# Layer 1's inverse square roots as powers on GpSimd, and a new order of the kernel's end (a two-layer graph network on one core)

## The chip, the core and the metric

The kernel runs on one core of a Trainium2 chip. The metric is the time of one execution on the device, in microseconds, and the figure given for a kernel is the median of its runs. A core has TensorE (PE, matrix products), VectorE (DVE), ScalarE (ACT), GpSimd (POOL) and SyncE (SP). Each works through its own queue of instructions in order, and an instruction that waits holds up all that stand behind it in that queue.

## What is computed

There are 4096 nodes with 64 features, an adjacency matrix of 4096 x 4096 zeros and ones, and two layers. Cut to what matters:

```python
def layer0(x):                      # a weighted sum of the neighbours
    rank = cumsum(mask, axis=1);  deg = rank[:, -1:];  k = minimum(deg, 100)
    pos = rank - (deg - k)
    w = mask * where(pos > 0, 0.5 ** (k - pos), 0.0)
    return w @ (x @ weight) + bias

def layer1(x):
    h = (adj @ x + x) / (sum(adj, axis=1) + 1)
    out = relu(concat([x, h], axis=1) @ W + b)
    return out / maximum(norm(out, axis=1), 1e-12)

x = layernorm(x + layer0(x))        # layernorm: (y - mean) / sqrt(var + 1e-5)
x = layernorm(x + layer1(x))
```

Layer 1 needs two inverse square roots for each node: one of the sum of squares of its `out` (the norm), and one of the variance of its row (the layernorm).

## The kernel before

**Tiles and stages.** The nodes are cut into eight slabs of 512 rows (four blocks of 128). The first 220 us or so are a pipeline over all (slab, k) pairs: it loads the adjacency in pieces of 128 x 4 x 512, counts neighbours, makes the weights of layer 0 and gathers; in between it finishes layer 0 for the slab before, and takes the parts of layer 1's sums whose rows are ready. The order within it is written out with hooks. The end, everything from `gather(*held)` (line 666) on, is written out by hand as a list of calls; a call puts its instructions into the queues of its engines, in the order of the list.

**The end.** Layer 1 is finished by units: slabs 5 and 2 (called 5_2), then 0 and 1 (0_1), 4 and 3 (4_3), slab 6, and slab 7 in two halves, 7a and 7b. For a slab, `own` (line 548) or `own_half` (553) runs TensorE over the remaining blocks of its sum, one matrix product for each. Then, for a unit:

- `last_hT` (563), for slab 7 `half_hT` (570): the sum is taken out of PSUM to hT, on VectorE where a stored part has to be added (L566), otherwise on ScalarE (L573).
- `last_pz` (588): TensorE multiplies hT by the weights (L594).
- `last_z` (596): VectorE adds the part of layer 1 that was computed before, c1 (L601).
- `last_sq` (603): the squares of relu(z), on ScalarE in two steps (L608, L609) or on VectorE in one (L611).
- `last_ss` (613): VectorE sums them (L616) and takes the larger of that and a floor (L618); ScalarE takes the square root (`root_a`, L364).
- `last_rn` (621): VectorE refines the root and inverts it (`root_b`): four small instructions, L370, L371, L373, L374.
- `last_y` (625): y = relu(z) times the inverse norm on VectorE (L630), plus x1 on GpSimd or VectorE (L633).
- `last_mv` (635): the mean and variance of y on VectorE (L382, L384); ScalarE takes the square root (L364).
- `last_r` (640): `root_b` again; with ScalarE next, VectorE also forms the offset, minus mean times inverse root (L646).
- `last_o` (648): the normalised rows, on ScalarE (L655, one instruction for each block of 128 rows) or VectorE (L659), and the store by SP (L664).

The two halves of an inverse root, as they stand before:

```python
s = sqrt(v + eps)                       # root_a, ScalarE
q = 1 / (s * s + eps + v)               # root_b, VectorE, three instructions
r = (s * 2.0) * q                       # root_b, VectorE, the fourth
```

**What ties the units together.** Most tiles of the end (hT, z, sq, y, and the small ones) have two buffers that units take in turn, so the third unit waits until the first has been read for the last time: y of 7a takes over the buffer of y of 4_3. GpSimd has no work in the end but its additions of x1. Its queue holds the loads of the adjacency before that.

Of the kernel before, what the change touches and what calls it, by code (L numbers as in the profile page):

```python
# [9 lines left out]
F32 = mybir.dt.float32  # L10
# [6 lines left out]
ALU = mybir.AluOpType  # L17
# [7 lines left out]
P = 128  # L25
R = 512
TB = R // P
# [6 lines left out]
LN_EPS = 1e-5  # L34
# [6 lines left out]
def adj_resnorm_kernel(  # L41
# [26 lines left out]
    nc = tc.nc  # L68
    D = w0.shape[0]
    NG, NK = adjT.shape[0], adjT.shape[1]  # L70
    NB = NK * KB
# [4 lines left out]
    const = ctx.enter_context(tc.tile_pool(name="const", bufs=1))  # L76
# [5 lines left out]
    small = ctx.enter_context(tc.tile_pool(name="small", bufs=2))  # L82
# [8 lines left out]
    for g in range(NG):  # L91
        n = 1 if g == 0 else 2 if g < 4 else 4
# [56 lines left out]
    zero = const.tile([P, 1], F32, name="zero")  # L149
    nc.vector.memset(zero, 0.0)  # L150
    eps_ln = const.tile([P, 1], F32, name="eps_ln")
# [36 lines left out]
    part = {}  # L188
    deg = const.tile([P, NB], F32, name="deg")
    least = const.tile([P, NB], F32, name="least")  # L190
    x1T = const.tile([D + 1, R], F32, name="x1T")
    nc.vector.memset(x1T[D : D + 1, :], 1.0)

# [112 lines left out]
    def second(acc, g, b, first, last):  # L306
        nc.tensor.matmul(acc, lhsT=x1hl[:, b, :], rhs=A[g][b // KB][:, b % KB, :], start=first, stop=last)  # L307
# [51 lines left out]
    ep = {}  # L359

    def root_a(v, eps, name):

        s = small.tile([P, v.shape[1]], F32, tag="s", name=f"s_{name}")
        nc.scalar.activation(s, v, AF.Sqrt, bias=eps)  # L364
        return s

    def root_b(s, v, eps, name):

        q = small.tile([P, v.shape[1]], F32, tag="q", name=f"q_{name}")
        nc.vector.tensor_tensor(q, s, s, ALU.mult)  # L370
        nc.vector.scalar_tensor_tensor(q, q, eps, v, ALU.add, ALU.add)  # L371
        r = small.tile([P, v.shape[1]], F32, tag="r", name=f"r_{name}")
        nc.vector.reciprocal(q, q)  # L373
        nc.vector.scalar_tensor_tensor(r, s, 2.0, q, ALU.mult, ALU.mult)  # L374
        return r

    def moments(y, name):
        n = y.shape[1]
        st = small.tile([P, n, 6], F32, tag="st", name=f"st_{name}")
        mv = small.tile([P, n, 2], F32, tag="mv", name=f"mv_{name}")  # L380
        for t in range(n):
            nc.vector.bn_stats(st[:, t, :], y[:, t, :])  # L382
        for t in range(n):
            nc.vector.bn_aggr(mv[:, t, :], st[:, t, :])  # L384
        return mv
# [122 lines left out]
    for c, chunk in enumerate(chunks):  # L508
        ahead = chunks[c + 1] if c + 1 < len(chunks) else []
        n, m = len(chunk), len(ahead)  # L510
# [5 lines left out]
        for (g, k), share in zip(chunk, shares):  # L516
# [7 lines left out]
            w = weigh(g, k, nr) if i == 0 else None  # L524
            for s in share:
                count(*s, s == ahead[0], s == ahead[-1])
            w = w or weigh(g, k, nr)
# [18 lines left out]
    a_half, b_half = slice(0, R // 2), slice(R // 2, R)  # L546

    def own(g, b0, b1):

        for b in range(b0, b1):  # L550
            second(acc[g], g, b, b == have[g] * KB, b == NB - 1)

    def own_half(rows, b0, b1):
        for b in range(b0, b1):
            nc.tensor.matmul(
                acc[L, rows.start],
                lhsT=x1hl[:, b, :],
                rhs=A[L][b // KB][:, b % KB, rows],
                start=b == 0,
                stop=b == NB - 1,  # L560
            )

    def last_hT(g):
        ep["hT", g] = epi.tile([P, R], F32, tag="hT", name=f"hT1_{g}")
        if g in part:
            nc.vector.tensor_tensor(ep["hT", g], acc[g], part[g], ALU.add)  # L566
        else:
            nc.scalar.copy(ep["hT", g], acc[g])

    def half_hT(rows):  # L570
        if rows.start == 0:
            ep["hT", L] = epi.tile([P, R], F32, tag="hT", name=f"hT1_{L}")
        nc.scalar.copy(ep["hT", L][:, rows], acc[L, rows.start])  # L573
# [22 lines left out]
    def last_z(u):  # L596

        name, bs = u
        z = ep["z", name] = epi.tile([P, len(bs), D], F32, tag="z", name=f"z_{name}")
        for t, c in spans(bs):  # L600
            nc.vector.tensor_tensor(z[:, t, :], ep["pz1", name][:, t, :], c1[:, c, :], ALU.add)  # L601

    def last_sq(u, on_act):
        name, bs = u
        z = ep["z", name]
        sq = ep["sq", name] = epi.tile([P, len(bs), D], F32, tag="sq", name=f"sq_{name}")
        if on_act:
            nc.scalar.activation(sq, z, AF.Relu)  # L608
            nc.scalar.activation(sq, sq, AF.Square)  # L609
        else:  # L610
            nc.vector.scalar_tensor_tensor(sq, z, 0.0, z, ALU.max, ALU.mult)  # L611

    def last_ss(u):
        name, bs = u
        ss = ep["ss", name] = small.tile([P, len(bs)], F32, tag="ss", name=f"ss_{name}")
        nc.vector.tensor_reduce(ss, ep["sq", name], AX.X, ALU.add)  # L616
        for t, c in spans(bs):
            nc.vector.tensor_tensor(ss[:, t], ss[:, t], least[:, c], ALU.max)  # L618
        ep["sn", name] = root_a(ss, zero, f"n_{name}")

    def last_rn(u):
        name, bs = u
        ep["rn", name] = root_b(ep["sn", name], ep["ss", name], zero, f"n_{name}")

    def last_y(u, on_pool):
        name, bs = u
        n = len(bs)
        y = ep["y1", name] = epi.tile([P, n, D], F32, tag="y", name=f"y1_{name}")
        rn = ep["rn", name].unsqueeze(2).to_broadcast([P, n, D])
        nc.vector.scalar_tensor_tensor(y, ep["z", name], 0.0, rn, ALU.max, ALU.mult)  # L630
        engine = nc.gpsimd if on_pool else nc.vector
        for t, c in spans(bs):
            engine.tensor_tensor(y[:, t, :], y[:, t, :], x1[:, c, :], ALU.add)  # L633

    def last_mv(u):
        name, bs = u
        mv = ep["mv1", name] = moments(ep["y1", name], f"l1_{name}")
        ep["s1", name] = root_a(mv[:, :, 1], eps_ln, f"l1_{name}")

    def last_r(u, on_act):  # L640
        name, bs = u
        mv = ep["mv1", name]
        r = ep["r1", name] = root_b(ep["s1", name], mv[:, :, 1], eps_ln, f"l1_{name}")
        if on_act:
            off = ep["off", name] = small.tile([P, len(bs)], F32, tag="off", name=f"off_{name}")
            nc.vector.scalar_tensor_tensor(off, mv[:, :, 0], -1.0, r, ALU.mult, ALU.mult)  # L646

    def last_o(u, on_act):
        name, bs = u
        y, mv, r = ep["y1", name], ep["mv1", name], ep["r1", name]  # L650
        o = wp.tile([P, len(bs), D], F32, tag="w", name=f"o_{name}")
        for t in range(len(bs)):
            if on_act:
                off = ep["off", name]
                nc.scalar.activation(  # L655
                    o[:, t, :], y[:, t, :], AF.Identity, bias=off[:, t : t + 1], scale=r[:, t : t + 1]
                )
            else:
                nc.vector.tensor_scalar(  # L659
                    o[:, t, :], y[:, t, :], mv[:, t, 0:1], r[:, t : t + 1], ALU.subtract, ALU.mult  # L660
                )
        for t, c in spans(bs):
            g, c0 = divmod(c.start, TB)
            nc.sync.dma_start(out=out[g][:, c0 : c0 + c.stop - c.start, :], in_=o[:, t, :])  # L664
# [36 lines left out]
    u = unit(5, 2)  # L701
# [3 lines left out]
    last_sq(u, True)  # L705
    last_hT(0)
    last_ss(u)
    own(1, 16, NB)
    last_rn(u)
    last_hT(1)  # L710
    last_y(u, True)
    own(4, 16, 24)

    v = unit(0, 1)
    last_pz(v)
    own(4, 24, NB)
    last_z(v)
    last_sq(v, True)
    last_mv(u)
    last_ss(v)  # L720
    last_hT(4)
    last_r(u, True)
    last_o(u, True)
    acc[3] = acc_of(3, "acc0")
    own(3, 12, NB)
    last_rn(v)
    last_y(v, True)
    last_hT(3)
    acc[6] = acc_of(6, "acc1")
# [2 lines left out]
    u = unit(4, 3)  # L732
    last_pz(u)
    last_mv(v)
    last_z(u)
    last_sq(u, True)
    last_r(v, True)
    last_ss(u)
    last_o(v, True)
    own(6, 20, NB)  # L740
    last_rn(u)
    last_y(u, True)
    last_hT(6)
    acc[L, 0] = acc_of(L, "acc0", R // 2, "7a")
    own_half(a_half, 0, NB // 2)
    last_mv(u)

    v = unit(6)
    last_pz(v)
    own_half(a_half, NB // 2, NB)  # L750
    last_r(u, True)
    last_z(v)
    last_sq(v, False)
    last_ss(v)
    half_hT(a_half)
    last_o(u, True)
    last_rn(v)
    last_y(v, True)
    acc[L, R // 2] = acc_of(L, "acc1", R // 2, "7b")
    own_half(b_half, 0, NB // 2)  # L760

    u, w = half_unit(0), half_unit(1)
    last_pz(u)
    own_half(b_half, NB // 2, NB)
    last_z(u)
    last_sq(u, False)
    last_ss(u)
    last_mv(v)
    last_rn(u)
    last_y(u, False)  # L770
    half_hT(b_half)
    last_pz(w)
    last_r(v, True)
    last_o(v, True)
    last_z(w)
    last_sq(w, False)
    last_ss(w)
    last_mv(u)
    last_rn(w)
    last_y(w, False)  # L780
    last_r(u, True)
    last_o(u, True)
    last_mv(w)
    last_r(w, False)
# [34 lines left out]
```

## Time and profile before

| what | us |
|---|---|
| median of 3 runs | 272.93 (272.83 to 273.19) |
| the profiled execution, whole | 273.33 |
| its span, first to last instruction | 271.5 |
| TensorE busy | 237.3 (87% of the span) |
| VectorE busy | 176.3 (65%) |
| ScalarE busy | 157.9 (58%) |
| GpSimd busy | 61.9 (23%) |

The profile is that of one execution. Busy time is a sum over the whole span; a line of the slices gives the busy share of an engine in each fortieth of the span, in tenths. A line of the timeline gives the start in us, the busy time in us, the engine, the line of the kernel, the operation, what it writes and what it reads, shapes, and how many instructions are merged; in brackets stands how long the engine had been idle before, and what released it. Names lose their slab numbers where the profile cuts them, so that "y" or "z" can be any unit; 7a and 7b keep theirs. The chain of work that ended last is followed back from the last instruction to what released each step; "issue" in it is time in which an engine waited for nothing that the profile shows.

### The profile page before, as it was taken

What the parts mean: (1) busy time and instruction counts of PE and PEld (TensorE: products, weight loads), DVE (VectorE), ACT (ScalarE), POOL (GpSimd) and SP (SyncE); (2) the same over time, 40 slices, a digit from 0 to 9 for tenths busy, and PEclk for the clock granted to TensorE, in tenths of its full rate; (3) what the DMA queues carried; (4) which work ended last, traced back from release to release, by engine and by line L of the source; (5) the groups of instructions that cost most, each with busy time, mean ns of one, the idle gap of its engine ahead of it and who ended that gap; (6) DMA issues with size and microseconds to landing.
All of it is one profiled execution on the core that took longest, in us unless ns stands there. A gap on an engine that the chain in (4) does not pass through costs nothing.

```text
span 271.5 us, 4838 instructions
## 1 busy us (share of the span) xinstructions
PE 237.3 (87%) x1865; PEld 105.0 (39%) x1865; DVE 176.3 (65%) x480; ACT 157.9 (58%) x226; POOL 61.9 (23%) x111
## 2 busy tenths in 40 slices
PE   8397688979899999999899999999998999997820
PEld 2122124334434343443344344434343546555710
DVE  5566634875596778367846684576577456597884
ACT  4456627897798869768854463436545322146351
POOL 8565551231101320322122121210200000221100
PEclk9979959999999999999999999999999999999985
DMA  6999999999997999799999999990500000010010
GB/s 97 195 230 234 241 212 214 222 214 214 223 214 141 165 211 214 124 171 214 182 179 205 203 162 180 168 168 12 98 2 0 0 2 0 0 42 20 19 58 21
DMA packets 12072, 37.13 MB, mean 137 GB/s; under 512 B 2066, under 2 KB 3218, under 8 KB 12050
## 3 DMA queue, kind: packets, MB, share of 16 engines
q0 software_dynamic: 10128, 35.66, 68.1%
q1 hardware_dynamic: 1922, 1.18, 1.5%
q8 instruction: 14, 0.23, 0.3%
q14 instruction: 8, 0.07, 0.1%
HBM read 69.34 MB, written 1.05 MB: 259 GB/s over the span
## 4 chain that ended last, share of the span: by engine, by line
PE 51%; DVE 11%; ACT 8%; issue 3%; POOL 1%; DVEq 0%; POOLq 0%; ACTq 0%
PE acc L298 10%; PE acc_part L307 9%; PE v L270 8%; PE v L280 5%; ACT w L287 4%; PE acc_right L307 3%; DVE w L288 3%; PE cnt L237 3%; PE vb L307 3%; PE pu L447 2%; PE va L307 2%; PE pz L594 2%; PE pz L395 2%; DVE x L422 1%; ACT a L320 1%
## 5 line engine op out<-in xcount | busy, mean ns | idle before, releaser
L288 DVE TENSOR_SCALAR w<-v 128x1024 int16<-128x1024 f32 x64 | 78.2, 1222 | 45.3 <-PE v L280 45.2
L287 ACT ACTIVATE w<-v,less 128x1024 int16<-128x1024 f32 x64 | 71.3, 1114 | 56.9 <-PE v L280 39.9
L298 PE MATMUL acc<-w,xhl 128*128 128x512 bf16 x256 | 67.2, 385 | 2.4 <-ACT hT L389 2.1
L109 POOL DMA_DIRECT2D a<-in_adjT_dram x65 | 35.5, 548 | 122.1 <-PE acc_part L307 49.9
L270 PE MATMUL v<-a,tri 64*64 64x512 bf16 x512 | 42.0, 397 | 4.3 <-ACT w L287 2.6
L298 PEld LDWEIGHTS <-xhl 128*128 128x128 f16 x256 | 23.9, 99 | 32.5 <-issue 9.5
L320 ACT CAST a<-a 128x1024 fp8e4<-128x1024 bf16 x32 | 33.3, 1039 | 0.0
L307 PEld LDWEIGHTS <-x1hl 128*128 128x128 f16 x224 | 19.8, 98 | 27.0 <-issue 5.7
L307 PE MATMUL acc_part<-a,x1hl 128*128 128x512 bf16 x108 | 28.0, 381 | 1.8 <-ACT x1hl L434 1.3
L247 DVE TENSOR_TENSOR cs<-cnt,cs 128x512 bf16<-128x512 f32 x20 | 13.8, 691 | 20.5 <-PE cnt L237 20.4
L237 PE MATMUL cnt<-a,pick 128*32 128x512 bf16 x256 | 21.9, 399 | 6.0 <-DMA a<-in_adjT_dram 6.0
L280 PE MATMUL v<-near,mine 32*128 32x512 bf16 x256 | 25.7, 391 | 0.2 <-ACT near L257 0.2
L270 PEld LDWEIGHTS <-tri 64*64 64x64 bf16 x512 | 12.6, 106 | 30.2 <-issue 28.0
L257 ACT ACTIVATE near<-rep,most 128x512 bf16<-128x512 f32 x28 | 19.1, 682 | 3.8 <-PE rep L255 3.7
L633 POOL TENSOR_TENSOR y<-y,x 128x256 f32<-128x256 f32 x7 | 5.0, 726 | 56.1 <-DVE y L630 56.1
L280 PEld LDWEIGHTS <-mine 32*128 32x128 bf16 x256 | 6.5, 91 | 24.9 <-issue 24.9
L255 PE MATMUL rep<-cs,further 128*128 128x512 bf16 x28 | 11.2, 400 | 3.7 <-DVE cs L247 1.7
L307 PE MATMUL acc_right<-a,x1hl 128*128 128x512 fp8e4 (+1 forms) x56 | 12.7, 379 | 0.0
L237 PEld LDWEIGHTS <-pick 128*32 128x32 bf16 x256 | 4.6, 94 | 19.8 <-issue 11.5
L655 ACT ACTIVATE o<-y,off,r_l 128x64 f32<-128x64 f32 x28 | 9.7, 428 | 3.1 <-issue 1.7
L382 DVE BATCH_NORM_STATS2 st_l<-y 128x6 f32<-128x64 f32 x60 | 9.0, 214 | 0.7 <-POOL y L633 0.6
L427 ACT CAST x1hl<-x 128x256 f16<-128x256 f32 x8 | 3.2, 406 | 10.1 <-DVE x L422 10.1
(139 smaller groups left out, 238.6 us busy)
## 6 DMA issues: line engine op xcount, KB each, us to landing
a<-in_adjT_dram POOLq DMA_DIRECT2D x63, 512.0 KB, 9.7
c<-in_x_pairs_dram POOLq DMA_DIRECT2D x8, 128.0 KB, 11.6
x<-in_x_dram POOLq DMA_DIRECT2D x8, 128.0 KB, 7.9
out_dram<-o SPq DMA_DIRECT2D x7, 128.0 KB, 1.7
a<-in_adjT_dram POOLq DMA_DIRECT2D x2, 256.0 KB, 4.7
out_dram<-o_7a SPq DMA_DIRECT2D x1, 64.0 KB, 1.9
out_dram<-o_7b SPq DMA_DIRECT2D x1, 64.0 KB, 1.5
w_sb<-in_L_gnn_weight_dram SPq DMA_DIRECT2D x2, 16.0 KB, 6.5
```

The source lines that it names most:

```text
L109: nc.gpsimd.dma_start(out=a[:, qs, :], in_=adjT[g, k][:, qs, :])
L237: nc.tensor.matmul(cnt[g][q * 32 : (q + 1) * 32, :], lhsT=pick[:, PW - 2 * k : PW - 2 * k + 32], rhs=A[g][k][:, q, :], start=first, stop=last,
L247: nc.vector.tensor_tensor(new, cnt[g], cs[g], ALU.add)
L255: nc.tensor.matmul(pr, lhsT=further, rhs=cs[g], start=True, stop=True)
L257: nc.scalar.activation(near[g], pr, AF.Relu, bias=most, scale=-1.0)
L270: nc.tensor.matmul(v[i][halves[c], r, :], lhsT=tri[halves[r], :], rhs=A[g][k][halves[r], 2 * i + c, :], start=True, stop=False,)
L280: nc.tensor.matmul(v[i][:, r, :], lhsT=mine[rows, 2 * k : 2 * k + 2, :], rhs=nr[rows, :], start=False, stop=True,)
L287: nc.scalar.activation(w[:, 0:2, :], v[0], AF.Relu, bias=less)
L288: nc.vector.tensor_scalar(w[:, 2:4, :], v[1], -STEP * MAX_NEIGH, 0.0, ALU.add, ALU.max)
L298: nc.tensor.matmul(acc0[g], lhsT=xhl[:, b, :], rhs=w[:, q, :].bitcast(BF16), start=(k, q) == (NK - 1, 0), stop=(k, q) == (0, KB - 1),)
L307: nc.tensor.matmul(acc, lhsT=x1hl[:, b, :], rhs=A[g][b // KB][:, b % KB, :], start=first, stop=last)
L320: nc.scalar.copy(kept[g, k][:, qs, :], A[g][k][:, qs, :], saturate=False)
```

## The change

Layer 1's inverse roots, but for those of unit 7b, are computed on GpSimd in one instruction, v to the power -0.5 (`root_p`; for the layernorm with an addition of eps ahead of it). The offset then is made on GpSimd too, as a product and a change of sign. ScalarE's square root and VectorE's four instructions are gone for these units. For 7b, the square root moves from `last_ss` and `last_mv` to `last_rn` and `last_r`. In the list of calls, steps change places: statistics or z of another unit are put between a sum and the use of its root, slab 6's x1 is added on VectorE instead of GpSimd, and slab 7a's sum is broken for slab 6's `last_pz` after 8 blocks instead of 16. The queue of TensorE is otherwise the same.

```diff
+    power = const.tile([P, 2 * TB], F32, name="power")
+    nc.vector.memset(power, -0.5)
...
+    def root_p(v, eps, name, tag):
+
+        n = v.shape[1]
+        r = small.tile([P, n], F32, tag=tag, name=f"{tag}_{name}")
+        if eps:
+            nc.gpsimd.tensor_scalar(r, v, eps, None, ALU.add)
+            v = r
+        nc.gpsimd.tensor_tensor(r, v, power[:, 0:n], ALU.pow)
+        return r
...
-        ep["sn", name] = root_a(ss, zero, f"n_{name}")
-
-    def last_rn(u):
+
+    def last_rn(u, on_pool):
         name, bs = u
-        ep["rn", name] = root_b(ep["sn", name], ep["ss", name], zero, f"n_{name}")
+        ss = ep["ss", name]
+        if on_pool:
+            ep["rn", name] = root_p(ss, None, name, "rn")
+        else:
+            ep["rn", name] = root_b(root_a(ss, zero, f"n_{name}"), ss, zero, f"n_{name}")
...
-        mv = ep["mv1", name] = moments(ep["y1", name], f"l1_{name}")
-        ep["s1", name] = root_a(mv[:, :, 1], eps_ln, f"l1_{name}")
-
-    def last_r(u, on_act):
+        ep["mv1", name] = moments(ep["y1", name], f"l1_{name}")
+
+    def last_r(u, on_pool):
         name, bs = u
         mv = ep["mv1", name]
-        r = ep["r1", name] = root_b(ep["s1", name], mv[:, :, 1], eps_ln, f"l1_{name}")
-        if on_act:
-            off = ep["off", name] = small.tile([P, len(bs)], F32, tag="off", name=f"off_{name}")
-            nc.vector.scalar_tensor_tensor(off, mv[:, :, 0], -1.0, r, ALU.mult, ALU.mult)
+        if not on_pool:
+            s1 = root_a(mv[:, :, 1], eps_ln, f"l1_{name}")
+            ep["r1", name] = root_b(s1, mv[:, :, 1], eps_ln, f"l1_{name}")
+            return
+        r = ep["r1", name] = root_p(mv[:, :, 1], LN_EPS, name, "r1")
+        off = ep["off", name] = small.tile([P, len(bs)], F32, tag="off", name=f"off_{name}")
+        nc.gpsimd.tensor_tensor(off, mv[:, :, 0], r, ALU.mult)
+        nc.gpsimd.tensor_scalar(off, off, -1.0, None, ALU.mult)
```

The list of calls, from unit 5_2 on:

```diff
     last_ss(u)
+    last_rn(u, True)
     own(1, 16, NB)
-    last_rn(u)
     last_hT(1)
     last_y(u, True)
...
     last_pz(v)
     own(4, 24, NB)
+    last_mv(u)
+    last_r(u, True)
     last_z(v)
     last_sq(v, True)
-    last_mv(u)
+    last_hT(4)
     last_ss(v)
-    last_hT(4)
-    last_r(u, True)
+    last_rn(v, True)
     last_o(u, True)
     acc[3] = acc_of(3, "acc0")
     own(3, 12, NB)
-    last_rn(v)
     last_y(v, True)
...
     u = unit(4, 3)
     last_pz(u)
     last_mv(v)
+    last_r(v, True)
     last_z(u)
     last_sq(u, True)
-    last_r(v, True)
-    last_ss(u)
     last_o(v, True)
     own(6, 20, NB)
-    last_rn(u)
-    last_y(u, True)
+    last_ss(u)
+    last_rn(u, True)
     last_hT(6)
     acc[L, 0] = acc_of(L, "acc0", R // 2, "7a")
-    own_half(a_half, 0, NB // 2)
-    last_mv(u)
+    own_half(a_half, 0, NB // 4)
 
     v = unit(6)
     last_pz(v)
-    own_half(a_half, NB // 2, NB)
-    last_r(u, True)
+    own_half(a_half, NB // 4, NB)
     last_z(v)
     last_sq(v, False)
+    last_y(u, True)
     last_ss(v)
+    last_rn(v, True)
     half_hT(a_half)
-    last_o(u, True)
-    last_rn(v)
-    last_y(v, True)
     acc[L, R // 2] = acc_of(L, "acc1", R // 2, "7b")
     own_half(b_half, 0, NB // 2)
+    last_y(v, False)
+    last_mv(u)
+    last_r(u, True)
+    last_o(u, True)
 
     u, w = half_unit(0), half_unit(1)
     last_pz(u)
     own_half(b_half, NB // 2, NB)
+    last_mv(v)
+    last_r(v, True)
     last_z(u)
     last_sq(u, False)
     last_ss(u)
-    last_mv(v)
-    last_rn(u)
-    last_y(u, False)
+    last_rn(u, True)
     half_hT(b_half)
     last_pz(w)
-    last_r(v, True)
     last_o(v, True)
+    last_y(u, False)
     last_z(w)
     last_sq(w, False)
     last_ss(w)
     last_mv(u)
-    last_rn(w)
+    last_r(u, True)
+    last_rn(w, False)
     last_y(w, False)
-    last_r(u, True)
     last_o(u, True)
     last_mv(w)
     last_r(w, False)
```

## The prediction

> **What bounds the kernel now.** I read the slices of the page, then busy time by stretch, then the timeline of the end, then the chain of work that ended last.
>
> ```profile
> PE   8397688979899999999899999999998999997820
> DVE  5566634875596778367846684576577456597884
> ```
>
> A slice is 6.8 us. TensorE is full up to the 37th slice; the last three have VectorE at 8, 8 and 4. The same by stretch (columns: length, busy PE, PEld, DVE, ACT, POOL, clock, DMA):
>
> ```profile
> 220.00:245.00 25.00, 25.00 (x147) 15.02 (x146) 15.91 (x71) 7.77 (x19) 2.82 (x4) 1.00 0.04 12
> 245.00:260.00 15.00, 11.21 (x88) 8.39 (x86) 12.19 (x61) 8.28 (x25) 2.14 (x3) 1.00 0.09 32
> 260.00:271.50 11.50, 0.66 (x4) 0.52 (x4) 6.92 (x38) 3.20 (x11) 0.00 (x0) 0.62 0.09 28
> ```
>
> Up to 245 TensorE never pauses: VectorE work removed there is worth nothing by itself. After 245 VectorE sets the pace and GpSimd is idle. The timeline names the places (start, length, engine, line):
>
> ```profile
> 249.86 0.68 DVE L566 TENSOR_TENSOR hT<-acc_right,part 128x512 f32<-128x512 f32 x1
> ...
> 250.59 1.10 PE L594 MATMUL pz<-wn_sb,hT 128*128 128x64 f32 x8 [1.39 <-DVE hT L566]
> ...
> 255.89 0.35 ACT L573 COPY hT<-acc_right_7a 128x256 f32<-128x256 f32 x1
> 256.14 2.76 ACT L655 ACTIVATE o<-y,off,r_l 128x64 f32<-128x64 f32 x8
> ...
> 257.47 0.73 POOL L633 TENSOR_TENSOR y<-y,x 128x256 f32<-128x256 f32 x1 [5.95 <-DVE y L630]
> 257.54 0.81 DVE L611 SCALAR_TENSOR_TENSOR sq_7a<-z_7a 128x128 f32<-128x128 f32 x1
> ...
> 259.95 0.35 ACT L573 COPY hT<-acc_right_7b 128x256 f32<-128x256 f32 x1
> ```
>
> TensorE waits 1.39 us for slab 6's hT, which stands on VectorE behind a root and a y, then for both halves of slab 7 (their copies stand behind roots on ScalarE). The last pieces of the chain:
>
> ```profile
> 260.30 1.72 issue
> 262.03 1.01 ACT o L655 x3
> ...
> 264.85 0.29 DVE y_7b L633
> 265.25 0.23 DVE q_l_7a L371
> ...
> 266.10 0.78 ACT o_7a L655 x2
> 266.92 0.30 ACT s_l_7b L364
> ```
>
> Between hT_7b and the end, VectorE's roots of other units (slab 6, 7a) stand in front of 7b's own steps; the last root of all, s_l_7b, starts at 266.92 behind o_7a.
>
> **What the skill says.** (1) GPSIMD Engine Reference, section 3.1: an fp32 add of 2048 columns takes 4497 ns on GpSimd. The trace has 726 ns for 256 (L633), so (4497-726)/1792 = 2.1 ns a column and 187 ns fixed: an 8-column step is about 0.20 us, an estimate; no row shows one. (2) The same page, section 7: a dependent fp32 chain costs 4 cycles a step at 1.2 GHz. No run here shows it. (3) SBUF — State Buffer, "Who interferes with whom": a VectorE instruction with two SBUF inputs and a GpSimd one that reads SBUF exclude each other for the whole instruction. The trace agrees: sq_7a took 807 ns beside POOL's add against 292 for sq_7b alone. (4) GPSIMD Engine Reference, section 2.1: the first call of a freshly loaded library costs some 6 us. No row shows that pow needs it.
>
> **The change, part by part.** Removed from VectorE: ten roots (two each of 5_2, 0_1, 4_3, 6, 7a) of four instructions, start to start 0.20+0.26+0.24+0.20 = 0.9 us, and five offsets of 0.17: some 9.8 us. After 245 lie seven of the roots and four offsets, 7.0 us. ScalarE loses ten square roots of 0.30. Added to GpSimd: ten pow; for the five statistics also an add of eps, a product and a negation, each waiting for the one before. Slab 6's add of x moves from POOL (0.73) to VectorE (0.42). No DMA moves past another; SP's stores follow the o they belong to. The memset of power (0.06, as its neighbours) lies in a 0.16 us gap of VectorE at 7 us: nothing.
>
> The unknown is pow. Below: the price of an add, 0.2 us for 8 columns. A gain beyond that is excluded, since pow does more than an add. Middle: logarithm, product and exponential as some 30 dependent steps (my count) of 4 cycles are 120 cycles = 0.1 us a column: 1.0 us for 8, 0.6 for 4, 0.4 for 2. Above: three times that, 3 us; a loop over 16 lanes one by one would be 13 us, which I leave outside the range. I take 1.0. Between dependent POOL steps I put 0.08 us; it could be 0.2.
>
> Now the order after, from rows of before. Up to ss_4_3 (ends 247.97) TensorE is full in both. For the earlier units pow must only keep ahead of TensorE: rn_5_2 comes at 231.2 (ss ends 230.05, hand-over to POOL 0.14 as at L633, pow 1.0) and y stands behind hT_1 until 232.6 anyway. The statistics of 5_2 now stand ahead of z_0_1 (0.6 later than 235.41), and rn_0_1 comes at 240.4, still ahead of where y_0_1 began before (240.96). z_4_3 begins at 244.91 in both, when TensorE gives pz_4_3; VectorE is through by 243.8.
> - hT_6 goes straight after ss_4_3: 247.9 to 248.6. pz_6 is now behind 8 of slab 7's matmuls, which end at 248.2: TensorE waits 0.4 instead of 1.39, and pz_6 ends at 249.5.
> - z_6, sq_6 (0.42+0.43) to 250.4, y_4_3 to 251.0. Its pow ran 248.1 to 249.1, so z_6 hides it, with 1.2 us to spare.
> - POOL adds x to y_4_3, 251.2 to 252.6. rn_6, needed next, is queued behind them on POOL: 252.6 to 253.2 (ss_6 was ready by 252). VectorE waits for it.
> - y_6 and its add 0.85: 254.1. Statistics of 4_3 (1.10+0.63 as for 5_2, less 0.1 overlap) to 255.7.
> - POOL: eps, pow, product, sign: 0.2+1.0+0.2+0.2, three gaps and the hand-over 0.14: 257.65. o_4_3 on ScalarE, 8 x 0.343: to 260.5. Before it began at 256.14. The copy of hT_7b is queued behind it: 260.5, against 259.95 before, though its sums are complete at 256.1 (258.7 before). So TensorE's waits vanish but **their gain is lost at this copy**: +0.55. y_7a is held by the same o_4_3, whose y buffer it takes over.
> - From hT_7b on: copy 0.35, pz_7b 0.45: z_7b at 261.4 (before 261.86, behind the roots of 7a and 6). sq, ss, max, square root and root of 7b: 0.32+0.32+0.20+0.35+0.95 = 2.15, so 263.6 (before 264.53); on VectorE the statistics of 7a hide under the square root, 0.3 looks out: 263.9. y and its add 0.6; no root of 7a behind it: statistics 0.6, to 265.1 (before 266.54).
> - s_l_7b stands behind o_7a. POOL's chain for 7a starts at 263.1: 0.2+0.4+0.2+0.2+0.24 = 1.25 and some 0.25 of contention: 264.6; o_7a 0.78: 265.4. s_l_7b starts at 265.4 instead of 266.92: **-1.5 us**. Root, o_7b and store follow as before.
>
> The profiled execution took 273.33 (span 271.5 and 1.83 around it), so 271.8; the median of the runs is 0.40 below it, 272.93: **271.4**.
>
> How it scales: a pow longer by d on 8 columns adds d at r_4_3, 0.5 d at rn_6, 0.25 d at r_7a: 1.75 d. Break-even is d = 1.5/1.75 = 0.86, so 1.86 us. At 0.3 us pow the sum is -2.7. If pow is 1.0 whatever its columns, rn_6 adds 0.4 and r_7a 0.6: -0.5. Gaps of 0.2: three each for 4_3 and 7a, +0.7 at most. Contention on root instructions of 7b against POOL's 7a chain: 0 to +0.6, I have 0.25.
>
> **Rivals.**
> 1. *Pow is slow and replaces VectorE's roots as the bound* (slower). At 3 us POOL's queue becomes the chain: y_0_1 waits until 242.4, its x adds end at 244.7, its statistics at 245.9 and hold z_4_3 1.1 late; r_0_1's chain runs 246.1 to 249.95, rn_4_3 stands behind it until 253, y_4_3 ends at 253.7 (+2.7); then rn_6 +1.0, r_4_3 +2.0, r_7a +0.5: +6.2-1.5 = +4.7, 277.6. Decides from 1.86 us. For it: 16 lanes to a core and a software function; against it: only that POOL is otherwise idle.
> 2. *The gain is given back*: pow of 1.5 to 2.1 us, or fixed in cost with long gaps: within 0.5 of 272.9. For it: hT_7b already waits longer than before.
> 3. *Pow is nearly an add*, 0.3: 270.2.
> 4. *First use costs 6 us*: rn_5_2 at 237.3 holds VectorE's queue (y, statistics, z_0_1, hT_4) 4.8 us. Of these VectorE's slack ahead of z_4_3 (244.9-243.8 = 1.1) takes 1.1, and 3.7 come through: 3.7-1.5 = +2.2, 275.1. Against it: POOL's adds show no such pause.
>
> That the change doesn't do what it says is no rival: the built program's order of instructions has the ten pow on POOL and the steps as moved.
>
> **How the numbers follow.** Forecast (pow 0.5 to 1.5) 0.45; pow below 0.5, 0.10; given back 0.15; slow pow 0.22, of which half beyond 276; first use 0.08. A measurement of this kernel tells 0.2%, 0.55 us, from no change. Faster 0.55 (forecast and rival 3), same 0.15, slower 0.30. The range goes from 270.1 (pow 0.3) to 276.0 (slow pow of about 2.6 us, first use); what lies outside is about 0.05 below and 0.11 above. The forecast alone: 270.6 to 272.4.
>
> **What would show it.** Right: pow of 128x8 near 1.0 us; TensorE's wait ahead of pz_6 below 0.6 and none ahead of pz_7a; o_4_3 starting near 257.7 and hT_7b straight behind it; s_l_7b about 1.5 us earlier than before. Wrong: pow of 2 us or more, VectorE's y waiting for POOL at each unit; or o_4_3 early enough that hT_7b is held by something else.

## The result

The changed kernel takes **276.29 us**, median of 4 runs (275.96 to 277.08), against 273.06 (272.83 to 273.31, 4 runs) for the kernel before: ratio 1.0122 (95% interval 1.0099 to 1.0146). It is slower by 3.2 us. The forecast was 271.4, and the range ended at 276.0.

The profiled execution took 277.08, with a span of 275.3 (before: 273.33 and 271.5). In it pz_5_2 (TensorE's product for the first unit), up to which TensorE's work is the same in both, starts at 225.63 instead of 224.84. In the kernels below whose first part is that of the kernel after, this start lies between 224.27 and 225.21, so I take the 0.79 as scatter of the first part. Without it the execution is 277.08 - 0.79 = 276.29, as the median. "Aligned" below means with such a shift taken off, or counted from pz_5_2.

Slices of the kernel after:

```profile
PE   8398669979899998999899999999988999999310
...
DVE  5547633875695678367756665675576655555551
...
POOL 8564551321101321231222121201100002765530
```

By stretch (columns: length, busy PE, PEld, DVE, ACT, POOL, clock, DMA share, GB/s):

```profile
220.00:245.00 25.00, 24.89 (x143) 14.75 (x142) 14.67 (x60) 6.59 (x15) 8.67 (x11) 1.00 0.03 11
245.00:260.00 15.00, 11.74 (x94) 9.11 (x93) 8.68 (x41) 4.48 (x12) 8.82 (x13) 1.00 0.05 18
260.00:275.30 15.30, 1.12 (x4) 0.93 (x4) 5.08 (x26) 5.43 (x17) 3.65 (x9) 0.56 0.10 34
```

VectorE was relieved as meant: between 245 and 260 it is busy 8.68 us instead of 12.19. Yet the last stretch is 3.8 us longer. Its timeline follows (start, length, engine, line, operation, tiles; in brackets the wait ahead of it). In these names rn is the inverse root for the norm and r that for the layernorm; s_l_7b is the last square root of all, for 7b's layernorm; pz is TensorE's product of a unit.

```profile
248.70 0.69 DVE L578 TENSOR_TENSOR hT<-acc_right,part 128x512 f32<-128x512 f32 x1
...
249.44 1.10 PE L606 MATMUL pz<-wn_sb,hT 128*128 128x64 f32 x8 [0.31 <-DVE hT L578]
...
253.58 1.02 POOL L386 TENSOR_TENSOR rn<-ss,power 128x4 f32<-128x4 f32 x1
254.63 0.43 DVE L645 SCALAR_TENSOR_TENSOR y<-z,rn 128x256 f32<-128x256 f32 x1 [1.68 <-POOL rn L386]
...
257.50 1.67 POOL L386 TENSOR_TENSOR r<-r,power 128x8 f32<-128x8 f32 x1
259.81 2.76 ACT L673 ACTIVATE o<-y,off,r 128x64 f32<-128x64 f32 x8 [6.24 <-POOL off L664]
...
262.48 0.35 ACT L585 COPY hT<-acc_right_7b 128x256 f32<-128x256 f32 x1
262.89 1.12 PE L606 MATMUL pz_7b<-wn_sb,hT 128*128 128x64 f32 x4 [5.84 <-ACT hT L585]
...
267.22 0.24 POOL L664 TENSOR_SCALAR off_7a<-off_7a 128x2 f32<-128x2 f32 x1
268.17 0.28 ACT L366 ACTIVATE s_l_7b<-mv_l_7b,eps_ln 128x2 f32<-128x2 f32 x1
269.90 0.33 SPq L682 DMA_DIRECT2D out_dram<-o_7b  x1
```

The order is the predicted one down to s_l_7b: TensorE's wait ahead of pz_6 fell from 1.39 to 0.31, and hT_7b stands right behind o_4_3. The sizes are not: the power of 8 columns takes 1.67, and pz_7b 1.12. The kernel before has its last store here:

```profile
268.66 0.33 SPq L664 DMA_DIRECT2D out_dram<-o_7b  x1
```

Aligned, the last store moved from 43.82 to 44.27 us after pz_5_2: **+0.45**. The span's end moved much more: it comes 271.52 - 268.66 = 2.86 after that store before, and 275.26 - 269.90 = 5.36 after: **+2.50**. No counted instruction starts in those 5.36 us behind the store's issue, and the chain of work that ended last stops ahead of it, at o_7b. The trace's records also hold instructions that the views do not count. Of GpSimd's end they have these (start us, operation, length ns):

```
before  257.469  TENSOR_TENSOR  727     (x onto y, the last arithmetic)
before  257.44   DRAIN         7449     ends 264.89
after   267.218  TENSOR_SCALAR  238     (sign of off_7a, the last arithmetic)
after   267.17   DRAIN         6986     ends 274.16
```

Behind its last arithmetic instruction GpSimd has a DRAIN, the last long instruction of its program, that ends 6.70 us after that instruction's end in both kernels. In the kernel before it is over at 264.89, long before the last store has landed (270.19). In the kernel after it ends at 274.16, when its last store had landed 2.7 us before (271.44), and the span ends 1.1 us behind the drain.

### The profile page after: what moved, and what is told of

It reads as the page before. It is cut to its first block, busy times and chain, and to the rows that moved or that the text cites. A ratio compares the mean times of both kernels' runs of the same rounds, so it can differ in the third digit from the quotient of the medians.

```text
span 275.3 us, 4776 instructions
## 1 busy us (share of the span) xinstructions
PE 235.6 (86%) x1836; PEld 105.5 (38%) x1865; DVE 169.0 (61%) x437; ACT 155.0 (56%) x216; POOL 78.1 (28%) x135
## 4 chain that ended last, share of the span: by engine, by line
PE 51%; DVE 9%; ACT 8%; issue 3%; POOL 2%; ACTq 0%; POOLq 0%; DVEq 0%
PE acc L300 10%; PE v L272 8%; PE acc_part L309 8%; PE v L282 4%; ACT w L289 4%; PE acc_right L309 3%; DVE w L290 3%; PE cnt L239 3%; PE vb L309 2%; PE pz L606 2%; PE pu L459 2%; PE va L309 2%; PE pz L407 2%; DVE x L434 1%; ACT a L322 1%
## 5 line engine op out<-in xcount | busy, mean ns | idle before, releaser
L300 PE MATMUL acc<-w,xhl 128*128 128x512 bf16 x242 | 64.8, 388 | 3.6 <-ACT hT L401 1.6
L309 PE MATMUL acc_part<-a,x1hl 128*128 128x512 bf16 x96 | 26.3, 381 | 2.5 <-ACT x1hl L446 1.3
L386 POOL TENSOR_TENSOR rn<-ss,power 128x8 f32<-128x8 f32 (+1 forms) x4 | 6.0, 1508 | 34.7 <-DVE ss L630 34.7
L673 ACT ACTIVATE o<-y,off,r 128x64 f32<-128x64 f32 x28 | 9.7, 431 | 7.1 <-POOL off L664 7.1
L620 ACT ACTIVATE sq<-z 128x512 f32<-128x512 f32 x3 | 1.9, 632 | 17.4 <-DVE z L613 17.4
```

What stands on the lines that cost most here:

```text
L300: nc.tensor.matmul(acc0[g], lhsT=xhl[:, b, :], rhs=w[:, q, :].bitcast(BF16), start=(k, q) == (NK - 1, 0), stop=(k, q) == (0, KB - 1),)
```

## The experiments

**Theory 1:** the program's end is the later of two times: the last store's issue plus 2.86 us, and the end of GpSimd's last arithmetic plus some 7.8 (6.70 of drain and 1.1). By moving r_7a's steps to GpSimd, the change put GpSimd's last work at 267.46 instead of 258.20, and its close on the path. **Rival:** the end follows the chain to s_l_7b alone, and the rest is chance. Beside that: is power's size the cause, or the order? All ratios are to runs of the kernel before on the same chip; differences in us to the kernel after are between medians.

### One addition on GpSimd, late and less late

Kernel before, and one 128x4 addition on GpSimd, whose result nobody reads. Its place is behind 7b's statistics in one kernel, and behind 7a's in the other:

```diff
     last_mv(w)
+    tiny = const.tile([P, 2, 2], F32, name="tiny")
+    nc.gpsimd.tensor_tensor(tiny, ep["mv1", "7b"], ep["mv1", "7b"], ALU.add)
     last_r(w, False)
```

> The kernel before, with one small extra GpSimd add (128x4, of slab 7b's moments, result unused) after 7b's statistics, that nobody waits for. Theory 1 (GpSimd's closing drain): in both traces the drain that ends GpSimd's program lasts until 6.70 us after its last arithmetic instruction, and the program ends 1.1 us later; the add ends near 266.9 of the span, so the span ends near 274.7 instead of 271.5: +3.1 us, about 276.1. The last store is issued at 268.7 as before. Theory 2 (the longer root steps alone account for the loss): the add is on no path, no change, 273.0. Theory 3 (a late instruction fetch or the number of GpSimd instructions): no change or a few tenths.

> The same extra add, but of 7a's moments, so that it ends near 263.8 of the span. Theory 1: drain until 270.5, end 271.6, just hidden behind the last store (issued 268.7, end 2.86 later): +0.0 to +0.3 us, 273.0 to 273.3. Theory 2: no change. If any late GpSimd arithmetic costs the same wherever it stands: as with the late add, +3.

Measured: late 275.95, ratio 1.0111 (1.0092 to 1.0131); less late 273.18, 0.9997 (0.9990 to 1.0004). Page and timeline of the late one:

```profile
span 274.1 us, 4810 instructions
...
266.37 0.20 POOL L785 TENSOR_TENSOR tiny<-mv_l_7b 128x4 f32<-128x4 f32 x1 [8.42 <-DVE mv_l_7b L384]
```

and of the other:

```profile
263.36 0.20 POOL L780 TENSOR_TENSOR tiny<-mv_l_7a 128x4 f32<-128x4 f32 x1 [5.35 <-DVE mv_l_7a L384]
```

An addition of 0.20 us that nobody waits for costs nothing at 263.4 and some 2.7 us at 266.4 (medians of 275.95 and 273.25 on that chip). In both, the last store is issued where it was (268.41 and 268.49). The drain ends at 273.27 and 270.26, again 6.70 behind each.

### Any instruction does it

Kernel before, with a memset of a dead tile on GpSimd as the very last call, behind 7b's o:

```diff
+    nc.gpsimd.memset(ep["mv1", "7b"], 0.0)
```

> The kernel before, with a GpSimd memset (128x4, of slab 7b's moments, after they have been read for the last time) as the last thing of all; nobody waits for it. It starts when o_7b has been written (268.7 of the span before) and takes 0.1 us. Theory 1 (the closing drain follows any last arithmetic of GpSimd by 6.7 us): GpSimd ends at 268.8, the span at 276.3 to 276.6: +4.8 to +5.1 us, about 278. If the drain is tied to an operation that reads, or to the power: no change, 273.

Measured: 278.12, 1.0184 (1.0159 to 1.0209).

```profile
span 276.3 us, 4839 instructions
...
268.70 0.10 POOL L786 MEMSET mv_l_7b<- 128x4 f32 x1 [10.55 <-DVE o_7b L659]
```

The drain ends at 275.50, 6.70 behind the memset's end at 268.80, and the span at 276.29. So neither power nor arithmetic is needed: 0.10 us of GpSimd work in the wrong place costs 5 us, more than the whole change.

### 7a's last root off GpSimd

The kernel after, with r_7a as square root and four instructions, off_7a on VectorE:

```diff
-    last_r(u, True)
+    last_r(u, False)
...
     last_rn(w, False)
```

> The changed kernel, with 7a's layernorm root and offset alone back on ScalarE and VectorE; GpSimd's last instruction is then rn_7a, near 262 of the span. Theory 1: the drain ends near 269 and is hidden; the end is set by the last store again, which I expect 0.3 to 0.7 us later than in the changed kernel because VectorE does 7a's root in front of 7b's: 274.5 to 274.9, so 1.4 to 1.8 us faster than the changed kernel and 1.5 to 1.9 slower than the one before. Theory 2: the end of the span stays 5.4 us behind the last store: 276.6 to 277.0.

Measured: 274.88, 1.0066 (1.0051 to 1.0081); 1.4 less than the kernel after.

```profile
span 272.9 us, 4778 instructions
...
270.06 0.33 SPq L685 DMA_DIRECT2D out_dram<-o_7b  x1
```

The span ends 2.88 after the store again (before: 2.86). The drain, over at 268.45, is hidden. But the store itself is later: aligned 45.18 against 44.27 in the kernel after, more than the 0.3 to 0.7 expected, since the root of 7a is back in front of 7b's steps. Of the 2.5 us at the close, 0.9 are given back there.

### Power at the price of a product

The kernel after, with a product in place of each power: it leaves out the inverse roots, and only its times count.

```diff
-        nc.gpsimd.tensor_tensor(r, v, power[:, 0:n], ALU.pow)
+        nc.gpsimd.tensor_tensor(r, v, power[:, 0:n], ALU.mult)
```

> The changed kernel with the power replaced by a product on the same operands: leaves out the inverse roots, every instruction and wait else stays. It takes GpSimd's steps from 1.67, 1.03 and 0.72 us (8, 4, 2 columns) to about 0.2. Theory 1 and 2: the last store is issued 2.8 us earlier. Theory 1: the end is still set by GpSimd, 7.8 us after the last instruction, which moves from 267.5 to about 264.6: about 273.4, no better than before although the last store is issued earlier than before. Theory 2: the end follows the store: 271.0 or less.

Measured: 273.68, 1.0013 (1.0004 to 1.0021).

```profile
span 271.3 us, 4776 instructions
...
259.80 0.66 PE L606 MATMUL pz_7b<-wn_sb,hT 128*128 128x64 f32 x4 [3.67 <-ACT hT L585]
...
265.98 0.33 SPq L682 DMA_DIRECT2D out_dram<-o_7b  x1
```

The last store is 3.0 us earlier than in the kernel after and 2.6 earlier than before (aligned 41.26 against 44.27 and 43.82), and the time is still no better than before. GpSimd's last instruction ends at 263.55, the drain at 270.25. So the prediction's cheapest case (270.2) was out of reach too: the close takes back what a free power would give.

### Order alone, roots alone

The kernel after with all roots as square root and VectorE's four instructions (order alone); and the kernel before's list of calls with the roots on GpSimd, the functions as after (roots alone).

```diff
     # order alone (r is made from v likewise):
-            ep["rn", name] = root_p(ss, None, name, "rn")
+            ep["rn", name] = root_b(root_a(ss, zero, f"n_{name}"), ss, zero, f"n_{name}")
...
-        nc.gpsimd.tensor_tensor(off, mv[:, :, 0], r, ALU.mult)
-        nc.gpsimd.tensor_scalar(off, off, -1.0, None, ALU.mult)
+        nc.vector.scalar_tensor_tensor(off, mv[:, :, 0], -1.0, r, ALU.mult, ALU.mult)
```

> The changed kernel's order of steps, all roots and offsets on ScalarE and VectorE as before. GpSimd's last addition of x then ends near 257 and its drain is hidden. Theory A (the order was made for roots that are off VectorE; alone it is a loss, since a unit's square root on ScalarE now stands behind 8 instructions of another unit's o, and VectorE waits for it at once): +4 to +7 us against the kernel before, 277 to 280. Theory B (the order carries a gain of its own that pow then spends): no slower than before, 273.0 or less.

> The list of steps of the kernel before, with the roots and offsets as powers on GpSimd (not 7b's). Theory A (the loss comes from roots on GpSimd late in the program, through the drain): GpSimd's last instruction ends near 266, the span near 273.7: +1.6 to +2.4 us, 274.7 to 275.5, and the last store is issued within 0.7 of the kernel before. Theory B (the new order lost it): within 0.5 of the kernel before, 272.5 to 273.5.

Measured: order alone 281.03, 1.0294 (1.0279 to 1.0308); roots alone 274.30, 1.0046 (1.0023 to 1.0069). The order costs 7.9 by itself, the roots 1.2, both together 3.2: they don't add. Order alone lies 1 us beyond the 277 to 280 expected; roots alone lies between its two expected ranges, since the last store comes 0.7 us earlier than before (aligned 43.11) and GpSimd's work ends earlier than was expected. Timeline of order alone:

```profile
248.27 2.74 ACT L672 ACTIVATE o<-y,off,r_l 128x64 f32<-128x64 f32 x8
...
250.93 0.28 ACT L366 ACTIVATE s_n<-ss,zero 128x8 f32<-128x8 f32 x1
...
252.77 1.97 PE L606 MATMUL pz<-wn_sb,hT 128*128 128x64 f32 x8 [4.51 <-DVE hT L578]
```

In this order hT_6 stands behind the root of 4_3 on VectorE, the root waits for its square root, and that stands behind o_0_1 on ScalarE: TensorE waits 4.51 and then multiplies at half pace (granted clock 0.50; 1.97 us for eight products that took 1.10 before). The order is made for roots that need neither engine. Waits of roots alone (engine and what waited, what for: us in all, times, longest):

```profile
DVE y L645 <- POOL rn L386: 7.3, 3, 3.0
```

With before's order VectorE stands 7.3 us, in three waits, for roots that it would have formed in 0.9 us each. GpSimd's last instruction ends at 264.63, and the drain (over at 271.33), not the store (268.04), ends the program.

### Roots alone, without 7a's

```diff
     # roots alone, and for unit 7a (whose offset is then formed on VectorE):
-    last_rn(u, True)
+    last_rn(u, False)
...
-    last_r(u, True)
+    last_r(u, False)
```

> The list of steps of the kernel before, roots as powers on GpSimd for all units but 7a and 7b. GpSimd's last instruction then ends 2 to 3 us earlier than with 7a's powers there, so the drain ends with or before the last store. Theory A (roots off VectorE are a gain that only the drain hides): 272.5 or less. Theory B (in the old order VectorE waits for pow about as long as it saves, since nothing stands between a sum and the use of its root): 273.0 to 274.4.

Measured: 274.54, 1.0052 (1.0026 to 1.0078), just beyond the second range. The drain is hidden (269.39, and the store landed at 270.74), and nothing is gained: the store, issued 0.7 us earlier than before in roots alone, is back (aligned 43.99). VectorE's waits for rn are the same 7.3 us in three. They are not all. The wait for the root of 4_3 also holds hT_6, and TensorE with it; roots alone has, and this kernel 0.28 later:

```profile
251.66 1.12 PE L606 MATMUL pz<-wn_sb,hT 128*128 128x64 f32 x8 [2.36 <-DVE hT L578]
...
252.60 3.58 PE L567 MATMUL acc_right_7a<-a,x1hl 128*128 128x256 bf16 x16
```

TensorE waits 2.36 (1.39 before), and from 252.6 on its granted clock is 0.50 for 3.4 us: 16 products take 3.58, which took 1.91 before. How much of the time goes to VectorE's waits and how much to this clock was not separated.

### TensorE kept busy

The kernel after, with 24 products in front of pz_7b, into a buffer that is read no more:

```diff
     own_half(b_half, NB // 2, NB)
+    for i in range(24):
+        nc.tensor.matmul(va[:, 0, :], lhsT=x1hl[:, 0, :], rhs=A[L][0][:, 0, :], start=True, stop=True)
```

> The changed kernel with 24 more products of 512 columns on TensorE (into a PSUM tile that nobody reads) after slab 7's sums: 5.2 us of work in the 5.8 us in which TensorE waits for hT_7b. If TensorE's half clock after that wait is what made pz_7b take 1.12 us instead of 0.66: pz_7b back to 0.66, all that follows it 0.5 earlier, GpSimd's last instruction too, 275.8 (0.3 to 0.6 less than the changed kernel). If the clock has another cause: pz_7b stays near 1.1 and the time near 276.3, or later by what the products overrun.

Measured: 275.67, 1.0104 (1.0087 to 1.0121); 0.6 less than the kernel after. The runs of the two overlap (275.24 to 276.29 and 275.96 to 277.08), so the trace is the better evidence.

```profile
255.52 5.34 PE L784 MATMUL va<-a,x1hl 128*128 128x512 bf16 x24
...
261.51 0.66 PE L606 MATMUL pz_7b<-wn_sb,hT 128*128 128x64 f32 x4 [0.65 <-ACT hT L585]
```

Work that nobody needs makes pz_7b 0.46 shorter (0.66 instead of 1.12) and the last store 0.49 earlier (aligned 43.78 against 44.27).

### The copy of 7b in front of o_4_3

The kernel after, with `last_o` of 4_3 behind `half_hT(b_half)`, and buffers of their own for y of 7a and 7b:

```diff
-    last_o(u, True)
...
     half_hT(b_half)
+    last_o(o43, True)     # o43: unit 4_3
```

> The changed kernel, with o of 4_3 put behind the copy of hT_7b on ScalarE, and buffers of their own for y of 7a and 7b; the same roots on the same engines. Theory A (the copy behind o_4_3 is what holds slab 7b, as the prediction said): hT_7b near 256.5 instead of 261.7 (counted as in the kernel before), the last store 3 us or more earlier; GpSimd then sets the end. Theory B (z_7b stands on VectorE behind y_7a, which waits for rn_7a, and that stands on GpSimd behind the chains of 4_3 and 6; the two waits end together): the copy and pz_7b are early, z_7b is not; 275.6 to 276.3, 0 to 0.7 us less than the changed kernel.

Measured: 275.44, 1.0079 (1.0059 to 1.0100); 0.85 less than the kernel after, a little more than the 0 to 0.7 of the second theory.

```profile
256.23 0.37 ACT L585 COPY hT<-acc_right_7b 128x256 f32<-128x256 f32 x1 [3.51 <-PE acc_right_7b L567]
...
261.68 0.29 DVE L646 SCALAR_TENSOR_TENSOR y_7a<-z_7a,rn_7a 128x128 f32<-128x128 f32 x1 [3.67 <-POOL rn_7a L386]
...
262.21 0.28 DVE L613 TENSOR_TENSOR z_7b<-pz_7b,c 128x128 f32<-128x128 f32 x1
```

Aligned, the copy comes 5.4 us earlier, but z_7b only 1.0: it stands behind y_7a on VectorE, and y_7a waits for its power, the last in GpSimd's queue behind r_4_3 and r_6. The copy behind o_4_3 was one of two waits that end together.

### An order made for both

From 4_3 on, an order that is to have each power beside work of VectorE, to block ScalarE nowhere, and to be done with GpSimd early. Powers remain for r_0_1, rn_6, r_4_3 and rn_7a; rn_4_3, r_6, r_7a and both of 7b go to ScalarE's square root (A) and VectorE (B), called apart; y of 7a and 7b have their own buffers. Units 5_2 and 0_1 up to there are as in the kernel after. The middle of the list:

```python
last_r(V6, A); last_pz(A7); own_half(b_half, NB // 2, NB); last_z(A7)
last_r(U43, P); last_sq(A7, False); last_ss(A7); half_hT(b_half)
last_rn(A7, P); last_pz(B7); last_r(V6, B); last_o(U43, True)
last_z(B7); last_y(A7, True); last_sq(B7, False); last_ss(B7)
```

> An order worked out by hand from the measured durations (pow 1.67, 1.03, 0.72 us; GpSimd's last instruction 7.8 us ahead of the end): roots as powers only where TensorE's or another unit's work covers them (5_2, 0_1, rn of 6, r of 4_3, rn of 7a), the others on ScalarE and VectorE; hT of 7b ahead of o of 4_3 on ScalarE; y of 7a and 7b in buffers of their own; GpSimd ends near 259. If the drain, the size of pow and the copy of hT_7b behind o_4_3 are the whole cause: last store issued near 264.5, the end near 267.3 of the span: 268 to 270, 3 to 5 us faster than before. If something else costs in the end (as a fixed price of arithmetic on GpSimd there): 272 or more.

Measured: **268.51** (268.35 to 268.78, 5 runs), 0.9837 (0.9824 to 0.9849): 4.6 us faster than before, 7.8 faster than after.

```profile
span 266.4 us, 4811 instructions
...
253.66 1.79 POOL L386 TENSOR_TENSOR r<-r,power 128x8 f32<-128x8 f32 x1
...
256.00 0.37 ACT L585 COPY hT<-acc_right_7b 128x256 f32<-128x256 f32 x1 [0.82 <-PE acc_right_7b L567]
...
256.43 0.66 PE L606 MATMUL pz_7b<-wn_sb,hT 128*128 128x64 f32 x4 [0.46 <-ACT hT L585]
257.69 0.45 POOL L651 TENSOR_TENSOR y_7a<-y_7a,x 128x128 f32<-128x128 f32 x1 [0.90 <-DVE y_7a L648]
...
263.52 0.37 SPq L690 DMA_DIRECT2D out_dram<-o_7b  x1
```

The power of 4_3 is as slow as ever (1.79), but nothing near it waits for it. TensorE waits 0.46 ahead of pz_7b, and GpSimd's last instruction is the addition at 257.69: the drain ends at 264.84, hidden.

### The same order, these four roots on VectorE

Is it the order alone?

```diff
-    last_r(U43, P)        # likewise r of 0_1, rn of 6 and 7a
+    last_r(U43, A)
+    last_r(U43, B)
```

> The new order (e7) with four of its powers (r of 0_1, rn of 6, r of 4_3, rn of 7a) back on ScalarE and VectorE at the same places in the list; the three earliest stay on GpSimd. If powers whose wait is covered are what makes the new order fast: 3 to 4.5 us slower than e7, 271.5 to 273. If the order alone makes it: within 1 us of e7, 268 to 269.5.

Measured: 273.33, 1.0009 (1.0000 to 1.0018): 4.8 slower than with powers, where 3 to 4.5 was expected. In these lists of calls the gain needs both, an order and powers that it covers:

| order | the roots in question by ScalarE and VectorE | by power on GpSimd |
|---|---|---|
| of before | 273.06 | 274.30 |
| of after | 281.03 | 276.29 |
| the new one | 273.33 | 268.51 |

In the first two rows it is all ten roots, in the third only the four named (the earlier units' stay on GpSimd in both). One rival stands: in this last kernel each of the four square roots is called directly in front of VectorE's part, and VectorE also stands 1.29 us (to 262.58) in r_6 until o_4_3 has been written. An order worked out for these roots on VectorE was not tried, so how much of the 4.8 is the powers' own is not shown.

### Theory 1 over all of them

Columns: last store's issue + 2.86; end of GpSimd's last instruction + 7.8; the span measured.

| kernel | store | GpSimd | span |
|---|---|---|---|
| before | 271.5 | 266.0 | 271.5 |
| after | 272.8 | 275.3 | 275.3 |
| late addition | 271.3 | 274.4 | 274.1 |
| less late | 271.4 | 271.4 | 271.4 |
| memset last | 271.5 | 276.6 | 276.3 |
| r_7a on VectorE | 272.9 | 269.6 | 272.9 |
| product for power | 268.8 | 271.4 | 271.3 |
| order alone | 279.2 | 265.6 | 279.3 |
| roots alone | 270.9 | 272.4 | 272.4 |
| roots alone, not 7a's | 272.1 | 270.5 | 272.1 |
| TensorE kept busy | 270.9 | 273.4 | 273.4 |
| copy first | 270.9 | 273.4 | 273.4 |
| new order | 266.4 | 265.9 | 266.4 |
| new order, VectorE | 271.6 | 271.7 | 271.7 |

The two constants are fitted on the kernels before and after; the other twelve come out within 0.35 us. The rival, an end that follows the store alone, misses six by 1.5 to 4.8 us and the kernel after by 2.5. In all fourteen traces the drain ends 6.70 us (6.695 to 6.703) after GpSimd's last instruction.

## Why the prediction was wrong

The mechanism of the chain was right nearly point by point, the sum had two terms of the wrong size, and one step, that the end follows the last store, failed. Times of after are aligned with the profiled execution of before (0.79 taken off).

| step | predicted | measured |
|---|---|---|
| hT_6 starts | 247.9 | 247.9 |
| wait ahead of pz_6 | 0.4 | 0.31 |
| wait ahead of pz_7a | none | none |
| y_4_3 ends | 251.0 | 251.3 |
| rn_6, length | 0.6 | 1.02 |
| 4_3's statistics to o_4_3 | 2.0 | 2.73 |
| o_4_3 starts | 257.7 | 259.02 |
| hT_7b starts | 260.5 | 261.69 |
| hT_7b's start to z_7b | 0.9 | 1.56 |
| s_l_7b starts | 265.4 | 267.38 |
| end after the last store | as before, 2.86 | 5.36 |

**Right:** VectorE's relief, hT_6 straight after ss_4_3, TensorE's waits gone, rn_6 behind the x additions on GpSimd with VectorE waiting for it, and "their gain is lost at this copy". That last was half the story: with the copy moved ahead, y_7a's wait for its power takes its place, and the time falls by 0.85 only.

**Mis-sized, the pow.** Predicted 1.0, 0.6 and 0.4 us for 8, 4 and 2 columns. Groups of the kernel after by shape (busy, mean ns; idle time before and its releaser):

```profile
L386 POOL TENSOR_TENSOR rn<-ss,power 128x8 f32<-128x8 f32 x3 | 5.0, 1670 | 34.7 <-DVE ss L630 34.7
...
L386 POOL TENSOR_TENSOR rn<-ss,power 128x4 f32<-128x4 f32 x1 | 1.0, 1020 | 0.0
...
L386 POOL TENSOR_TENSOR rn_7a<-ss_7a,power 128x2 f32<-128x2 f32 x1 | 0.7, 719 | 0.0
...
L663 POOL TENSOR_TENSOR off<-mv_l,r 128x8 f32<-128x8 f32 x3 | 0.6, 203 | 0.2
```

That is some 0.40 us fixed and (1670-719)/6 = 159 ns a column. The estimate from the Trainium skill (GPSIMD Engine Reference, section 7: four cycles a dependent step) had 0.1 a column from my count of 30 steps, and nothing fixed. The estimate of 0.20 for an 8-column product from that page's section 3.1 was right: 203 ns. The power of 4 columns is 0.42 longer than predicted, that of r_4_3 0.67: 1.09 of the 1.19 by which hT_7b is late. By the prediction's own 1.75 d, with d = 0.67 on 8 columns, the end comes 1.2 later: 271.4 + 1.2 = 272.6, rival 2's "given back", and still not slower than before. Rival 1 (3 us) and rival 4 (a first use of 6 us) did not occur: the three 128x8 powers average 1.67, the first of them, rn_5_2, 1.68.

**Mis-sized, pz_7b.** Predicted 0.45 from its start to z. The kernel before already has 0.66 for these four products, with z_7b held by other steps:

```profile
260.36 0.66 PE L594 MATMUL pz_7b<-wn_sb,hT 128*128 128x64 f32 x4 [1.66 <-ACT hT L573]
```

So some 0.20 of the miss could be read there. The other 0.46 is the clock. In the kernel after TensorE had waited 5.84, its granted clock over the four products was 0.50, and they took 1.12. The prediction had this wait in its own figures (sums complete at 256.1, copy at 260.5) and put no price on it. hT_7b to z_7b is 0.66 longer by both together. The run with filler products shows the clock's part: granted clock 1.00, the products 0.66, and 0.49 at the store.

The Trainium skill (TensorE: Matmul & The Clock Gate, part 1, "What's actually happening") says that TensorE falls to half clock after an idle window of about 3.4 us. After waits of 5.84 and 4.51 (order alone) the traces agree, with a granted clock of 0.50. After 3.67 (product for power) it was still 1.00, and in roots alone it fell to 0.50 after a wait of 2.36. In these runs, then, the length of the wait alone does not tell whether the clock falls.

1.19 and 0.66 are 1.85 of s_l_7b's lateness of 1.98; the other 0.13 is spread over the steps from z_7b to s_l_7b.

**Failed: "Root, o_7b and store follow as before".** They did, but the prediction let the end of the program follow the store as before too (2.86), and it did not. The prediction costed GpSimd's steps only by who reads their results. Its work for 7a, ending at 267.46 instead of 258.20, also moved GpSimd's close, which had been hidden by 5.5 us. No step and no rival had it. It is worth 2.50 of the measured difference; the chain gives 0.45 (predicted -1.5, +1.95 for what is above); together 2.95 of 3.23 between the medians. The other 0.28 is nearly all (0.27) how far the profiled execution of before lies above its median (273.33 and 273.06).

The drain's part is shown by a kernel that changes nothing else (the late addition, the memset). What the 6.70 us consist of is not known. Whether they depend on the loads that GpSimd issues earlier was not tried.

## What to carry to other kernels

Before work is moved to an idle engine at a program's end, ask when that engine would be done and what it still has to do to close: here GpSimd's last instruction, however small, had to end some 5 us ahead of the last store's issue (7.8 less 2.86). A slow instruction on an idle engine paid here only where other work covered it. Order and place of the roots are one decision: either alone cost 1.2 to 7.9 us here, and together, in an order that covers the powers, they gained 4.6.

## What the runs showed of the hardware

- In all 14 traces GpSimd's long closing DRAIN ended 6.7 us after its last instruction, whether that was an addition, a power, a sign, or a memset of 0.10 us; the program ended 0.8 to 1.1 us later where nothing else was later.
- The power of fp32 on GpSimd: 1.67 us for 128x8, 1.02 for 128x4, 0.72 for 128x2, against 0.20 for a product and 0.24 to 0.27 for a tensor with a scalar (kernel after); dependent instructions there start 0.08 to 0.09 us after one another's end.
- Four products of 128x64 took 1.12 us at a granted clock of 0.50, after TensorE had waited 5.84 us, and 0.66 at 1.00, after 3.67. In roots alone the clock fell to 0.50 for 3.4 us after a wait of 2.36.
